# A decoder layer in fp32: tokens and context also handed over feature-major, one bank for new keys and values, gathers spread over the heads

## The chip, the cores and the metric

The kernel runs on one core of one Trainium2 chip. The metric is the device time of one execution in microseconds (us), the median of several runs. PE is TensorE, DVE is VectorE, ACT is ScalarE, POOL is GpSimd; SP and ACT and POOL also issue DMA transfers. A profile is one execution recorded by the hardware profiler.

## The reference, cut to what matters

One decoder layer on 2048 tokens (32 sequences of 64) of width 512: self-attention, cross-attention to a context of the same shape, and a feed-forward part, each followed by a layer norm.

```python
DIM, NH, NKV, HD = 512, 32, 8, 128
BLOCK, NBLK, TOPK = 32, 128, 16
q = rope(x @ wq.T); k = rope(x @ wk.T); v = x @ wv.T       # 32 query heads, 8 key heads
k_sel = k_cache[block_idx].reshape(-1, NKV, HD)            # 16 blocks of 32 rows = 512 cached keys
v_sel = v_cache[block_idx].reshape(-1, NKV, HD)
k_full = concatenate([k_sel, k[0]]); v_full = concatenate([v_sel, v[0]])   # + 64 new = 576 keys
attn = softmax(q @ k_full / sqrt(HD)); x = layernorm(x + (attn @ v_full) @ wo.T)
# cross-attention: q = x @ Wq + bq; k, v = split(context @ Wkv + bkv); per sequence of 64
x = layernorm(x + xattn(x, ctx) @ Wo + bo)
# feed-forward: z = x @ W.T + b, m = sum over 8 adapters of rank 16, z + min(0.5|z|/|m|, 1) * m
x = layernorm(x + ffn(x))
```

The new keys and values are those of the first sequence alone (`k[0]`, `v[0]`), and all 2048 tokens attend to the same 576 keys.

## The kernel before

Everything is fp32. The tokens are cut into four blocks of 512 (`NTB`), the heads into eight groups of four query heads that share one key head (`NKV`, `REP`). Self-attention is one long loop over `n`, 128 units of (group, token block, head). Its products with the large weights (queries, output projection) are done with seven quarter products instead of eight: a weight is loaded as four quarters, POOL makes the four sums that the scheme needs (`load_left`, `load_right`), POOL also makes four sums of the tokens (`token_sums`), and `Queries` and `Projection` issue the products 1 to 7 one at a time, in the order of `ORDER`.

In a unit, `scores(n, i)` is called four times, for 128 tokens each: two matmul pairs into a score bank (`s`, two banks in turn), DVE takes the row maximum (`nmax`), ACT the exponential and its sum (`p`, `den`), DVE the reciprocal, the multiplication of `p` and a 32 x 32 block transpose (`turn`, tile `T`). `move(n)` then has SP issue sixteen small transfers that bring `T` into the layout of `pT`, and two units later `values` multiplies it with `v` into the banks `po0` and `po1`. Between those matmuls, `step(place)` puts one query product of the next token block (`q_step`) or one output product of a past block (`w_step`) at each of four places of a unit: `steps = {0: "qwqw", 1: "qw q", 2: "wqwq", 3: "w qw"}[h]`. PE and DVE run in the order of the program, by hand; in the prologue (between `begin` and `begin.close()`) all engines do.

What the products need is the token matrix with features on the partitions (`xTs[tb]`), and it arrives token-major. So the kernel turns it on PE: `transpose_rows` does four 128 x 128 transposes against an identity into one bank and a copy by ACT or DVE out of it. For the first token block this is the beginning of the program; for blocks 1 to 3 the dictionary `early` spreads twelve such tiles over the first six units; every block is also written to DRAM (`xs`), and for later groups one transfer per block reads it back. The context is turned in the same way: four tiles in the last units (`pen0`), four after the loop (`en1`, bank `enbank`), eight in the key and value stage that follows (`rows_turn`, `pen2`, `pen3`).

Per group, when its second token block begins (`r == REP`), `gather_keys` and `gather_values` have POOL issue eight indirect transfers (four of keys, four of values, 128 rows each), `load_group` loads that group's key and value weights, `rotate` (a block later) applies the rotary factors on DVE and POOL, `new_keys` computes the new keys and values on PE, and `cached_keys` transposes the rotated keys on PE. `new_keys` uses the PSUM bank tag `po1` twice, once for the keys, read by ACT (L574), once for the values, read by ACT (L585).

When the output projection of a group's last token block has done its seventh product, `w_step` loads the next group's output weights into the same tiles: `load_right` issues four quarter loads on SP, then four POOL sums. The next group's first product (`w_0x`, `w_1x`... are banks of product 1 and 2 of block 0, 1...) is about three quarters of a unit later.

After the loop, `kv0` makes the keys and values of the first context block while the last output projections end. The key and value stage, cross-attention and the feed-forward part follow; the change touches the first of these only.

Of the kernel before, what the change touches and what calls it, by code (L numbers as in the profile page):

```python
# [16 lines left out]
P = 128  # L17
# [35 lines left out]
def decoder_layer(  # L53
# [3 lines left out]
    enc: bass.AP,  # L57
# [44 lines left out]
    def token_room(b, name):  # L102
        return act.tile([P, NC, TB], F32, tag=f"xT{b % 2}", name=name)

# [111 lines left out]
    def load_right(src, name, eng, queue=nc.sync):  # L216

        w = operands("wo", name)
        b12 = w[5]
        for dst, (k, n) in ((w[1], (0, 0)), (w[2], (1, 0)), (w[3], (1, 1)), (b12, (0, 1))):  # L220
            load_quarter(dst, src, k, n, queue)
        right_sums(eng, w[1], b12, w[2], w[3], {1: w[5], 2: w[6], 3: w[7], 4: w[4]})
        return w
# [191 lines left out]
    xs = [dram.tile([P, NC, TB], F32, name=f"xs{tb}") for tb in range(NTB)]  # L415
# [29 lines left out]
    def load_enc(tile_, tb, j):  # L445
        r0 = tb * TB + j * P
        nc.sync.dma_start(out=tile_, in_=enc[r0 : r0 + P, :])

# [6 lines left out]
    with ExitStack() as ph:  # L455
# [13 lines left out]
        blk = kc.tile([P, TOPK], I32, name="blk")  # L469
        nc.sync.dma_start(out=blk, in_=block_idx.partition_broadcast(P))  # L470
        for j in range(TPB):
            (nc.scalar if j % 2 else nc.sync).dma_start(
                out=acc[0][:, j, :], in_=x[j * P : (j + 1) * P, :]
            )
        wq0 = operands("wq", "wq0")
        for i, (k, m), queue in (
            (1, (0, 0), nc.sync), (4, (1, 1), nc.scalar),
            (5, (0, 1), nc.sync), (2, (1, 0), nc.scalar),
        ):
            load_quarter(wq0[i], wqT[:, : REP * HD], k, m, queue)  # L480
# [7 lines left out]
        NQ = P // BLOCK  # L488
        NKT = NSEL // P
        off_i = kc.tile([P, 1], I32, name="off_i")  # L490
        for q in range(NQ):
            nc.gpsimd.iota(
                off_i[q * BLOCK : (q + 1) * BLOCK, :], pattern=[[0, 1]], base=0,
                channel_multiplier=1,
            )
# [3 lines left out]
        blk_f = kc.tile([P, TOPK], F32, name="blk_f")  # L499
        nc.vector.tensor_copy(blk_f, blk)  # L500
        row_f = kc.tile([P, NKT], F32, name="row_f")
        for q in range(NQ):
            r = slice(q * BLOCK, (q + 1) * BLOCK)
            nc.vector.tensor_scalar(
                row_f[r, :], blk_f[r, :].rearrange("p (t q) -> p t q", q=NQ)[:, :, q],
                float(BLOCK * NKV), off[r, :], ALU.mult, ALU.add,
            )
        k_rows = k_cache.rearrange("n (h d) -> (n h) d", d=HD)
        v_rows = v_cache.rearrange("n (h d) -> (n h) d", d=HD)
        rows_cur, kn_cur, wkv_cur, kTs, vs = {}, {}, {}, {}, {}  # L510
# [11 lines left out]
        def gather_rows(g, dst, src):  # L522
            for t in range(NKT):
                nc.gpsimd.indirect_dma_start(
                    out=dst[:, t, :], out_offset=None, in_=src,
                    in_offset=bass.IndirectOffsetOnAxis(ap=rows_cur[g][:, t : t + 1], axis=0),
                )

        def gather_keys(g):
            rows_cur[g] = kv.tile([P, NKT], I32, tag="row", name=f"row{g}")  # L530
            nc.vector.tensor_scalar(rows_cur[g], row_f, float(g), None, ALU.add)
            kn_cur[g] = kv.tile([P, NKT, HD], F32, tag="kn", name=f"kn{g}", bufs=1)
            gather_rows(g, kn_cur[g], k_rows)

        def gather_values(g):
            vs[g] = kv.tile([P, NKC, HD], F32, tag="v", name=f"v{g}")
            gather_rows(g, vs[g], v_rows)

        def rotate(g):


            kn = kn_cur.pop(g).rearrange("p t (d two) -> p t d two", two=2)
            kr = kv.tile([P, NKT, HD], F32, tag="kr", name=f"kr{g}", bufs=1)
            k4 = kr.rearrange("p t (d two) -> p t d two", two=2)
            shape = [P, NKT, HD // 2]
            c3 = cs[:, None, :].to_broadcast(shape)
            s3 = sn[:, None, :].to_broadcast(shape)
            tmp = kv.tile(shape, F32, tag="tmp", name=f"kt{g}", bufs=1)
            tmq = kv.tile(shape, F32, tag="tmq", name=f"kq{g}", bufs=1)
# [7 lines left out]
            return kr  # L557
# [3 lines left out]
        def new_keys(g, tags=("po1", "po1")):  # L561

            wk, wv = wkv_cur.pop(g)
            src = xTs[0] if g == 0 else x64
            kTs[g] = kv.tile([P, NKEY], F32, tag="kT", name=f"kT{g}")
            pk = bank([P, 1, TB], f"pkn{g}", tags[0])[:, 0, :]
            for c in range(NC):
                nc.tensor.matmul(  # L570
                    pk[:, :SEQ], wk[:, c, :], src[:, c, :SEQ],
                    start=(c == 0), stop=(c == NC - 1),
                )
            nc.scalar.activation(  # L574
                kTs[g].rearrange("p (s b k) -> p s b k", s=2, k=SQ)[:, :, SHARED, :],
                pk[:, :SEQ].rearrange("p (s k) -> p s k", s=2), AF.Copy, scale=nrm2,
            )
            pv = bank([P, 1, TB], f"pvn{g}", tags[1])[:, 0, :]
            for c in range(NC):
                for i in range(2):  # L580
                    nc.tensor.matmul(
                        pv[i * SEQ : (i + 1) * SEQ, :HD], src[:, c, :SEQ], wv[:, c, :],
                        start=(c == 0), stop=(c == NC - 1), skip_group_check=True,
                    )
            nc.scalar.copy(vs[g][:, NKT, :], pv[:, :HD])  # L585

        def cached_keys(g, kr, tag="po1"):
# [13 lines left out]
        xTs = {}  # L601
# [86 lines left out]
        wq_cur, wo_cur, tok, qrs, pjs, reads = {}, {}, {}, {}, {}, []  # L688
        ORDER = (1, 2, 6, 7, 4, 5, 3)
# [12 lines left out]
        def q_step(n):  # L702

            b = n // REP + 1
            if b < NB:
                if b not in qrs:
                    start_queries(b, {k: "q" for k in "xyz"})
                    qrs[b].todo = list(ORDER)
# [3 lines left out]
                if i == 5:  # L712
                    reads.append(qrs[b].corner)

        def w_step(b):
# [5 lines left out]
            pj.step(pj.todo.pop(0))  # L721
            reads.append(pj.read)
            if not pj.todo:
                del pjs[b]
                g, tb, _ = units[b * REP]
                if tb == NTB - 1:
                    wo_cur[g + 1] = load_right(woT[columns(g + 1), :], f"wo{g + 1}", nc.gpsimd)
# [11 lines left out]
        for i in range(2):  # L739
            special[f"s{i}"] = sc.tile([P, 2, 512], F32, tag="sc", name=f"startbank{i}")[:, 0, :]  # L740
        xTs[0] = token_room(0, "xT0")

        def first_tile(j, tag):
            transpose_rows(acc[0][:, j, :], xTs[0], j, f"x_0_{j}", tag)

        sub = ALU.subtract
        q = {(i, j): xTs[0][:, quarter(i, j)[0], quarter(i, j)[1]]
             for i in range(2) for j in range(2)}
        t = {i: big.tile([P, 2, HF], F32, tag=f"tx{i}", name=f"tx0_{i}") for i in range(1, 5)}
        gather_keys(0)  # L750
        for j, tag in enumerate(("q", "w", "po0", "po1")):
            first_tile(j, tag)
        nc.vector.tensor_tensor(t[1], q[0, 1], q[0, 0], sub)
        nc.vector.tensor_tensor(t[2], q[1, 1], t[1], sub)
        nc.vector.tensor_tensor(wq0[7], wq0[1], wq0[5], sub)
        nc.vector.tensor_tensor(wq0[5], wq0[5], wq0[4], ALU.add)
        nc.vector.tensor_tensor(wq0[6], wq0[5], wq0[1], sub)
        wq_cur[0] = wq0
# [8 lines left out]
        nc.scalar.dma_start(out=acc[1], in_=rows(x, 1))  # L767
# [578 lines left out]
```

## Time and profile before

| | |
|---|---|
| median of 3 runs | 3136.03 us (3135.63 to 3137.8) |
| the profiled execution | 3155.39 us; its span from first to last instruction 3153.6 us |
| granted TensorE clock over the span | 0.994 |
| PE busy | 3081.5 us (98%) |
| DVE busy | 2200.4 us (70%) |
| POOL busy | 973.7 us (31%) |
| ACT busy | 771.2 us (24%) |

Durations of single instructions come from the profiled execution, whose own time is 19.4 us above the median. A line of a wait list names who waited, on what line, for whom, and then the total in us, the number of times and the longest. A line of the timeline has the start in us from the span's beginning, a length, engine, line, operation, output tile and inputs, shape and count; in brackets, how long the engine was idle before it and what released it. Matmuls are pipelined: what one costs is the time from its start to the next start. A wait for several semaphores is put down to the one that came last by the profile, so the name of a releaser can be wrong.

### The profile page before, as it was taken

The numbers are of one execution on the slowest core, as the hardware profiler recorded it, in microseconds if no ns is written. First come the engines' busy times: TensorE is split into PE (matmuls) and PEld (weight loads), VectorE is DVE, ScalarE is ACT, GpSimd is POOL, SyncE is SP. The second block draws the span as 40 slices with busy tenths as digits, with TensorE's granted clock in tenths as the row PEclk, the third lists the DMA queues.
The fourth block names the chain that finished last, engine by engine and source line by source line (L and its number), as shares of the span: only waits on it lengthen the run. The fifth ranks groups of instructions, "written<-read, shape, count | busy, mean of one in ns | idle before, by whom it ended". The sixth has DMA issues, their size and how long they took to land.

```text
span 3153.6 us, 42581 instructions
## 1 busy us (share of the span) xinstructions
PE 3081.5 (98%) x15072; PEld 2332.0 (74%) x15072; DVE 2200.4 (70%) x3945; ACT 771.2 (24%) x1782; POOL 973.7 (31%) x793
## 2 busy tenths in 40 slices
PE   8999999999999999999999999999999999999998
PEld 6677677677677676776777769988888888888864
DVE  6677777777777777777777754436666666656777
ACT  3323223222222222232232322211111111111122
POOL 3222222232222222223222113135434434444421
PEclk9999999999999999999999999999999999999999
DMA  5444444444444444444344443221121121121101
GB/s 186 118 113 113 118 107 122 111 113 113 115 122 108 115 125 109 104 127 115 96 125 110 111 114 121 107 94 48 54 61 50 52 61 52 49 65 50 48 27 41
DMA packets 187315, 298.70 MB, mean 95 GB/s; under 512 B 44128, under 2 KB 92768, under 8 KB 183008
## 3 DMA queue, kind: packets, MB, share of 16 engines
q1 hardware_dynamic: 173600, 281.46, 33.3%
q10 hardware_dynamic: 11072, 9.26, 1.0%
q0 software_dynamic: 2432, 5.26, 0.6%
q8 instruction: 122, 2.00, 0.3%
q14 instruction: 89, 0.73, 0.1%
HBM read 102.86 MB, written 25.17 MB: 41 GB/s over the span
## 4 chain that ended last, share of the span: by engine, by line
PE 91%; DVE 5%; SPq 1%; ACT 1%; issue 1%; DMA 1%; another core or an unknown queue 0%; ACTq 0%; DVEq 0%
PE po L656 15%; PE s L610 15%; PE sx L1068 2%; PE pox L1120 2%; PE wx_0y L268 1%; PE wx_2y L268 1%; PE wx_1y L268 1%; PE w_0y L268 1%; PE w_1y L268 1%; PE q_3y L268 1%; PE qx_3y L268 1%; PE qx_0y L268 1%; PE w_3y L268 1%; PE wx_3y L268 1%; PE q_1y L268 1%; PE q_0y L268 1%
## 5 line engine op out<-in xcount | busy, mean ns | idle before, releaser
L618 ACT ACTIVATE p<-s,nmax 128x576 f32<-128x576 f32 x512 | 379.8, 742 | 1186.2 <-DVE nmax L615 1145.9
L610 PE MATMUL s<-kT,qT 128*128 128x288 f32 x2048 | 579.0, 408 | 1.3 <-ACT p L618 1.3
L656 PE MATMUL po<-pT,v 128*128 128x512 f32 (+1 forms) x1280 | 551.9, 605 | 2.0 <-DVE encT L125 1.0
L610 PEld LDWEIGHTS s<-kT,qT 128*128 128x128 f32 x2048 | 388.3, 191 | 100.5 <-issue 19.1
L615 DVE TENSOR_REDUCE nmax<-s 128x1 f32<-128x576 f32 x512 | 384.3, 751 | 83.0 <-PE s L610 63.6
L636 DVE STREAM_TRANSPOSE T<-p 128x576 f32<-128x576 f32 x512 | 394.4, 770 | 4.4
L656 PEld LDWEIGHTS po<-pT,v 128*128 128x128 f32 (+1 forms) x1280 | 214.8, 190 | 203.2 <-issue 173.5
L628 DVE TENSOR_SCALAR p<-p,den 128x576 f32<-128x576 f32 x512 | 310.9, 607 | 17.9
L242 POOL TENSOR_TENSOR so<-oT,oT 128x512 f32<-128x512 f32 x32 | 42.4, 1326 | 726.3 <-ACT oT L679 726.3
L627 DVE RECIPROCAL den<-den 128x1 f32<-128x1 f32 x512 | 83.9, 164 | 236.2 <-ACT p L618 227.9
L244 POOL TENSOR_TENSOR so<-oT 128x512 f32<-128x512 f32 x32 | 40.7, 1273 | 320.3 <-PE w_1y L268 83.1
L1078 ACT ACTIVATE ex<-ex 128x512 f32<-128x512 f32 x64 | 40.4, 631 | 328.1 <-DVE ex L1077 328.1
L191 POOL TENSOR_TENSOR tx<-xT 128x512 f32<-128x512 f32 x31 | 39.8, 1283 | 236.6 <-PE q_1z L268 68.6
L1224 POOL TENSOR_TENSOR txx<-x1T 128x512 f32<-128x512 f32 x31 | 39.4, 1270 | 237.0 <-PE qx_3z L268 95.7
L618 ACT ACTIVATION_READ_ACCUMULATOR p<-s,nmax 128x1 f32 x512 | 99.0, 193 | 0.0
L1137 DVE TENSOR_SCALAR oTx<-pox,bv 128x256 f32<-128x256 f32 x128 | 56.1, 479 | 50.0 <-PE pox L1120 50.0
L242 POOL TENSOR_TENSOR sox<-oTx,oTx 128x512 f32<-128x512 f32 x32 | 40.5, 1267 | 156.8 <-DVE oTx L1137 151.8
L679 ACT COPY oT<-po 128x512 f32<-128x512 f32 x128 | 71.9, 587 | 43.5 <-PE po L656 42.5
L1068 PEld LDWEIGHTS sx<-kvx,qTx 128*64 128x64 f32 x2048 | 64.8, 138 | 20.9 <-issue 11.3
L1120 PE MATMUL pox<-pTx,kvx 64*128 64x256 f32 x512 | 74.5, 407 | 2.3 <-DMA pTx<-Tx 1.7
L1135 ACT ACTIVATE oTx<-pox,bv 128x256 f32<-128x256 f32 x128 | 53.8, 471 | 82.8 <-PE pox L1120 82.8
L1068 PE MATMUL sx<-kvx,qTx 128*64 128x64 f32 x2048 | 73.5, 225 | 0.0
(472 smaller groups left out, 5855.0 us busy)
## 6 DMA issues: line engine op xcount, KB each, us to landing
pT<-T SPq DMA_DIRECT2D x1020, 80.0 KB
pT<-T SPq DMA_DIRECT2D x1016, 64.0 KB
xT<-xs SPq DMA_DIRECT2D x28, 1024.0 KB
kvx<-kv SPq DMA_DIRECT2D x32, 512.0 KB
pTx<-Tx SPq DMA_DIRECT2D x256, 64.0 KB
kv<-c SPq DMA_DIRECT2D x30, 512.0 KB
xwq<-in_xwq SPq DMA_DIRECT2D x32, 256.0 KB
xwo<-in_xwo SPq DMA_DIRECT2D x32, 256.0 KB
```

What stands on the lines that cost most here:

```text
L242: nc.gpsimd.tensor_tensor(t[1], a[1, 0], a[1, 1], ALU.add)
L268: nc.tensor.matmul(self.banks[b][:, m, :], self.left[i][:, k, m * P : (m + 1) * P], self.right[i][:, k, :], start=(first and m + k == 0), ...
L610: nc.tensor.matmul(s[:, a, :HALF], qTs[n // REP][:, units[n][2], i * P : (i + 1) * P], kTs[g][:, a * HALF : (a + 1) * HALF], start=True, s ...
L615: nc.vector.tensor_reduce(nmax, s[:, :, :HALF], AX.XY, ALU.max, negate=True)
L618: nc.scalar.activation(p.rearrange("q (a k) -> q a k", a=2), s[:, :, :HALF], AF.Exp, bias=nmax, accum_out=den,)
L627: nc.vector.reciprocal(den, den)
L628: nc.vector.tensor_scalar(p, p, den, None, ALU.mult)
L636: nc.vector.transpose(Ts[n][:, :, i, :], ps_.pop((n, i)).rearrange("q (b k) -> q b k", k=SQ))
L656: nc.tensor.matmul(pos[n].rearrange("d (a q) -> d a q", a=NQD), vs[units[n][0]][rows, v, :], pTs[n // 2][rows, :, chunk, :], skip_group_ch ...
L679: nc.scalar.copy(o[:, i, :].rearrange("d (t a k) -> d a t k", t=TPB, a=NQD), pos.pop(n - 1 + i).rearrange("d (a t k) -> d a t k", a=NQD, t ...
L1068: nc.tensor.matmul(s[b * SEQ : (b + 1) * SEQ, i * REP + h, :], qTs[n][:, h, c0 : c0 + SEQ], kvs[n][:, pr, 0, c0 - pr * HF : c0 - pr * HF + ...
L1120: nc.tensor.matmul(po[b][:, i, :].rearrange("d (h a j) -> d h a j", h=REP, a=2), kvs[n][r, pr, 1, i * HD : (i + 1) * HD], pTs[n][r, :, t * ...
```

## The change

The host hands over `x` and the context transposed as well (`xT_in`, `encT_in`, 512 x 2048); `x` itself is still read for the residual sum. The index of the blocks is laid out on the host as 128 x 4.

- No tile of `x` or of the context is transposed on PE any more, `xs` and its stores are gone, and `load_features` loads a token block or context block as one transfer with features on the partitions.
- The prologue loads the first token block in quarters, makes the sums in another order, rotates the first keys in two halves, and leaves query product 3 to the first unit; products of the first two blocks stand at other places of the first three units, and block 1's use the bank tag `w` as well.
- `new_keys` puts new keys and new values into one bank, and ACT reads both after all matmuls.
- `load_right` is split: the first two quarters of the next group's output weights are loaded when products 1 and 2 of the group's last block are done, the other two when all seven are.
- The gathers go one per head: a key gather at the beginning and a value gather after the third score tile of each of the second block's four heads.
- At the end of self-attention the last products of `kv0` and the first two of the last projection alternate.

The core of the diff:

```diff
+    def load_features(dst, src, tb, queue=nc.sync):
+        queue.dma_start(
+            out=dst, in_=src[:, tb * TB : (tb + 1) * TB].rearrange("(c p) n -> p c n", p=P)
+        )
...
+    def load_right(src, name, eng, queue=nc.sync, first=None):
+        w = first or load_right_first(src, name, queue)
+        for i in range(3, 8):
+            w[i] = big.tile([P, 2, HF], F32, tag=f"wo{i}", name=f"{name}_{i}")
         b12 = w[5]
-        for dst, (k, n) in ((w[1], (0, 0)), (w[2], (1, 0)), (w[3], (1, 1)), (b12, (0, 1))):
+        for dst, (k, n) in ((w[3], (1, 1)), (b12, (0, 1))):
             load_quarter(dst, src, k, n, queue)
         right_sums(eng, w[1], b12, w[2], w[3], {1: w[5], 2: w[6], 3: w[7], 4: w[4]})
+        return w
+
+    def load_right_first(src, name, queue=nc.sync):
+        w = {i: big.tile([P, 2, HF], F32, tag=f"wo{i}", name=f"{name}_{i}") for i in (1, 2)}
+        for i in (1, 2):
+            load_quarter(w[i], src, i - 1, 0, queue)
         return w
...
+        for i, j, n, (k, m) in ((0, 0, 1, (0, 0)), (1, 0, 2, (1, 0)), (0, 1, 5, (0, 1)), (1, 1, 4, (1, 1))):
+            load_quarter(q[i, j], xT_in, i, j, (nc.sync, nc.scalar)[i and j])
+            load_quarter(wq0[n], wqT[:, : REP * HD], k, m, (nc.scalar, nc.sync)[n == 5])
...
-            pk = bank([P, 1, TB], f"pkn{g}", tags[0])[:, 0, :]
+            new = bank([P, 1, TB], f"new{g}", "po1")[:, 0, :]
+            pk, pv = new[:, :SEQ], new[:, P : 2 * P]
             (key matmuls)
-            (ACT reads the keys)
-            pv = bank([P, 1, TB], f"pvn{g}", tags[1])[:, 0, :]
             (value matmuls)
+            (ACT reads the keys)
             (ACT reads the values)
...
         def w_step(b):
...
+            if tb == NTB - 1 and g + 1 < NKV:
+                src, name = woT[columns(g + 1), :], f"wo{g + 1}"
+                if i == 2:
+                    wo_next[g + 1] = load_right_first(src, name)
+                if not pj.todo:
+                    wo_cur[g + 1] = load_right(src, name, nc.gpsimd, first=wo_next.pop(g + 1))
...
+        new_keys(0)
+        rotate(0, 0, NKT // 2)
+        nc.vector.tensor_tensor(c[1, 1], z, c[1, 0], ALU.add)
+        nc.vector.tensor_tensor(c[0, 1], y, c[1, 0], ALU.add)
+        rotate(0, NKT // 2, NKT)
+        for j in range(NKT):
+            gather_values(0, j)
+        cached_keys(0, "s0")
...
+        tok[1] = token_sums(xTs[1], "tx1", nc.gpsimd)
+        wo_cur[0] = load_right(woT[columns(0), :], "wo0", nc.gpsimd, first=wo_cur[0])
+        for tb in range(NTB):
+            (nc.scalar if tb else nc.sync).dma_start(out=acc[tb], in_=rows(x, tb))
...
             if r == REP and g + 1 < NKV:
-                gather_keys(g + 1)
-                gather_values(g + 1)
                 load_group(g + 1)
+            if r // REP == 1 and g + 1 < NKV:
+                gather_keys(g + 1, h)
...
+                if n < REP:
+                    i = {(0, 0): 3, (0, 1): 7, (0, 3): 4}.get((n, place))
+                    if i:
+                        last_products(i)
+                    elif (n, place) in ((0, 2), (1, 0), (1, 1), (1, 2), (1, 3), (2, 0), (2, 2)):
+                        q_step(n)
...
             step(2)
-            early_tiles(n, 2)
+            if r // REP == 1 and g + 1 < NKV:
+                gather_values(g + 1, h)
             scores(n, 3)
...
-                if NTB <= b + 3 < NB:
-                    xTs[b + 3] = token_room(b + 3, f"xT{b + 3}")
-                    nc.sync.dma_start(out=xTs[b + 3], in_=xs[units[(b + 3) * REP][1]])
+            if h == REP - 1 and b + 3 < NB or n == 0:
+                b2 = b + 3 if n else 2
+                xTs[b2] = token_room(b2, f"xT{b2}")
+                load_features(xTs[b2], xT_in, b2 % NTB)
...
-        kv_step(4, 3)
-        store_kv(0, 0, tiles)
-        spare2 = sc.tile([P, 2, 512], F32, tag="sc", name="enbank")
-        for j in range(TPB):
-            special["en"] = spare2[:, j % 2, :]
-            transpose_rows(en1[j], encT[1], j, f"pen1_{j}", "en")
+        pj.step(1)
+        pj.read()
+        kv_step(4)
+        pj.step(2)
+        pj.read()
+        kv_step(3)
+        store_kv(0, 0, tiles)
         encR[1] = token_sums(encT[1], "te1", nc.gpsimd, tag="so")
-        for i in KV_ORDER:
+        for i in (6, 5, 7, 3, 4):
```

Lines in parentheses stand for matmul loops and reads that are unchanged in themselves.

## The prediction

> **What bounds the kernel now.** I read the page first (shares, chain), then who waited for whom on PE, then the timeline and the stretches around each wait.
>
> ```profile
> span 3153.6 us, 42581 instructions
> PE 3081.5 (98%) x15072; PEld 2332.0 (74%) x15072; DVE 2200.4 (70%) x3945; ACT 771.2 (24%) x1782; POOL 973.7 (31%) x793
> PE 91%; DVE 5%; SPq 1%; ACT 1%; issue 1%; DMA 1%; another core or an unknown queue 0%; ACTq 0%; DVEq 0%
> ```
>
> TensorE is the chain (91%). So two things are worth time: matmul work that goes, and moments in which PE stands. The list of waits has nearly all of those moments:
>
> ```profile
> PE pvn L581 <- ACT kT L574: 11.9, 7, 1.7
> PE x L123 <- ACT xT L125: 10.6, 2, 5.3
> PE x L123 <- DMA acc<-in_x: 6.7, 1, 6.7
> PE w_0x L268 <- DMA wo<-in_woT: 3.9, 3, 1.5
> PE w_0x L268 <- DVE nmax L615: 3.0, 2, 1.5
> PE w_0x L268 <- DVE den L627: 2.6, 1, 2.6
> ```
>
> Columns: total us, times, longest. The change touches every row. Next the stretches (length, then busy time of PE, PEld, DVE, ACT, POOL, granted clock, DMA share, GB/s), for the first block of tokens (four heads), the start of the second, and one whole group of later work:
>
> ```profile
> 22.70:77.20 54.50, 46.44 (x191) 33.86 (x189) 42.37 (x71) 18.47 (x42) 20.86 (x20) 0.94 0.56 169
> 77.20:97.00 19.80, 14.47 (x55) 9.92 (x54) 10.64 (x20) 7.09 (x16) 9.96 (x10) 0.83 0.32 87
> 97.00:328.00 231.00, 229.31 (x907) 164.15 (x906) 176.53 (x313) 67.98 (x158) 55.81 (x46) 1.00 0.45 115
> 372.00:376.60 4.60, 4.45 (x22) 3.04 (x23) 1.71 (x4) 0.61 (x3) 0.00 (x0) 0.63 0.57 160
> ```
>
> The later group is PE-bound (229 of 231 us, DVE 177). The first 97 us are not: PE idles there and the clock falls (0.94, 0.83).
>
> **The change part by part.** The sum is made against the profiled execution, 3155.39 us; the median of the runs shown is 3136.03, 19.4 us less. I carry that difference over unchanged.
>
> *1. Token and context transposes go.* PE loses 32 tiles of four transposes: 16 of tokens, 16 of context. The 16 tiles of x1 stay. What a tile costs on PE is the start of its successor minus its own start:
>
> ```profile
> 82.66 0.60 PE L123 MATMUL x<-ident,acc 128*128 128x128 f32 x4
> 83.10 1.14 PE L610 MATMUL s<-kT,qT 128*128 128x288 f32 x4
> 92.69 0.90 PE L123 MATMUL x<-ident,acc 128*128 128x128 f32 x3 [5.33 <-ACT xT L125]
> ```
>
> 83.10 - 82.66 = 0.44 us. Twelve tiles lie in the first 97 us (items 4 and 5), 8 at the end of self-attention (item 6), and 8 in the key and value stage, where PE is never idle (1930 to 2096: 166.0 of 166.0): 8 x 0.44 = 3.5 us gained there. Their ACT and DVE copies were beside PE work: nothing.
>
> *2. New keys and values in one bank.* At each of seven groups PE waited between the key and the value products, because both used the tag po1:
>
> ```profile
> 139.97 1.00 PE L570 MATMUL pkn<-x,wk 128*128 128x64 f32 x8
> 142.67 1.09 PE L581 MATMUL pvn<-wv,x 128*64 128x128 f32 x16 [1.70 <-ACT kT L574]
> ```
>
> Eight matmuls of 0.105 us end near 140.8; the next start is 142.67: 1.86 us, seven times, 13.0 us. In the new order both products are issued before the ACT reads, and po1 is next written a head later, so nothing takes the wait's place. Two of the seven waits were followed by about 3.4 us at half clock (the row of 372.00 to 376.60 shows 0.63), 1.7 us lost each. The Trainium skill ("TensorE: Matmul & The Clock Gate", section on HAM oscillation) speaks against counting these: PE should avoid idle gaps above about 3.4 us, and 1.7 us is below. By rule 13.0 us, by trace 16.4. I take the trace, with 13.0 in the range.
>
> *3. Output weights in two steps.* SP now loads the first two quarters of the next wo after product 2 of the group's last block, some 3.5 heads (about 50 us) earlier; SP only waits there for that product, with nothing due behind it before the head's own move. Before, all four stood behind the sixteen moves of a head:
>
> ```profile
> 797.91 1.13 PE L610 MATMUL s<-kT,qT 128*128 128x288 f32 x4
> 801.62 1.97 PE L268 MATMUL w_0x<-wo,oT 128*128 128x256 f32 x8 [2.57 <-DVE den L627]
> ```
>
> The releaser named is wrong: it is the load, issued at 798.4. The three w_0x rows sum to 9.5 us in six waits; all go. What is late next are POOL's sums for product 6, due about 13 us later; they needed until 809.9 before, from a landing that now holds two loads instead of four. No new wait: 9.5 us.
>
> *4. Prologue and first block.* Before, the first scores started at 22.7 and those of the second block at 77.2. Now: the eight quarter loads are as many bytes as the tiles and weights before, and share their 8 DMA lanes, so product 1 starts as the transposes did, at 6.7. At half clock it takes 3.4, the ACT copy 0.6, product 2 2.0: 12.8. Then two products at 1.73, new keys and values 1.9: 18.1. DVE: six sums at 0.69 after the last weight quarter (about 11.5), 0.6 of small ones, two half rotations of about 1.5, two adds of 0.69: 19.8. Then transposes 0.6 and two ACT copies: first scores at about 21. This gains 1.7 although product 3 now comes after. The four heads hold 16 score pairs at 0.97, ten products at 1.73 and 8.0 of values, 40.8 us of PE. DVE has 4 x (0.75 + 0.16 + 0.61 + 0.77) = 9.2 a head and eight adds, 42.1 us. So DVE binds here; with 5 us for the links between engines the second block starts near 68, 9 us earlier. What made 54.5 us of this before was one DVE instruction:
>
> ```profile
> 40.38 3.76 DVE L628 TENSOR_SCALAR p<-p,den 128x576 f32<-128x576 f32 x1
> 41.32 1.28 POOL L190 TENSOR_TENSOR tx<-xT 128x512 f32<-128x512 f32 x1
> 46.76 0.47 PE L123 MATMUL x<-ident,acc 128*128 128x128 f32 x1 [5.30 <-ACT xT L125]
> ```
>
> It usually takes 0.52; ACT, then the tile's copy, then PE waited behind it. The Trainium skill ("GPSIMD Engine Reference", Specifications) says GpSimd shares its SBUF interfaces with VectorE and contends with two-port or two-input DVE instructions. This speaks against the change: eight POOL sums stand in a row (10 us), about 23 to 33, beside the DVE-bound heads. By rule each of some eight multiplies could wait one POOL sum, 8 x 1.28 = 10 us, and the 9 us are gone. By trace the mean multiply is 0.61 against 0.52. I take 0.61 and keep 0 as an end. The early loads (4 MB of rows, 3 of tokens) are at most 10.5 MB by about 36 us at the 330 GB/s seen here; the first values are due near 44. ACT's moves could wait 1 to 2 us on a lane: inside the 5 us.
>
> *5. Second block.* PE stood 5.33 us before a tile (row 92.69), then ran 6.8 us at half clock (3.4 lost); both hang on the tile's copy. With four tiles (1.8) that is 10.5 us. The seven late DVE reads at this place belong to the burst of eight gathers:
>
> ```profile
> DVE nmax L615 <- remote: 16.6, 7, 5.4
> ```
>
> In the other six groups PE lost nothing there. One pair of gathers per head moves 64 POOL issues of about 1 us off that burst, with three more row additions of 0.15 us on DVE a group; DVE has 50 us free in a group: nothing.
>
> *6. End of self-attention.* Eight tiles (3.5), the idle time between the last four (0.68 + 0.85 + 0.68 = 2.2), their half clock (w_3x took 2.85 against 1.89, and 0.5 in the tile: 1.5), and about 1.7 of waits on tile copies and on a value read that a reordered product now covers: 8.9 us. The single 1 MB loads of context start after the last readers of their room, 15 us or more ahead of use.
>
> *7. Feature-major loads each block.* They replace loads of the stored copy, at the same place on SP. Pieces are 2 KB instead of 8. The row loads of x have the same pieces and reached 360 GB/s; a block has four heads of slack: nothing. If they came later, the moves behind them on reused lanes would be late.
>
> Sum: 3.5 + 16.4 + 9.5 + 9 + 10.5 + 8.9 = 57.8 us. 3155.4 - 57.8 = 3097.6 in a profiled execution; 3136.0 - 57.8 = 3078.2 in the median. I say 3079.
>
> **The rivals.** *A. The start gives nothing* (DVE beside POOL, and half of item 5 comes back as DVE-bound waits): less 9 and 8.7: gain 40, 3096. For it: the multiply of 3.76. Against: DVE was busy only 42.4 of 54.5. *B. The early stalls belong to the profiled execution*, which is 19.4 us longer than the median: 5.3 + 3.4 of item 5 and as much of item 4 would not be in the median: again about 3096. *C. Slower: the gathers.* Late signals beside the gather burst (1.2 to 5.4 us) cost PE 5.3 us once. If each of the 28 heads that now gathers stopped PE so, 28 x 5.3 = 149 us, 3136 - 58 + 149 = 3227. It decides from 2.1 us a head. Against: no PE loss in six of seven bursts, and two gathers are not eight.
>
> **How the numbers follow.** Main case 0.70, its own range 3060 to 3094 (item 2 by rule, item 4 from 0 to 14). A 0.14, B 0.10, C 0.05, no measurable change 0.01. To hold eight in ten the range reaches over A and B: 3060 to 3102. 0.2% is 6.3 us, about what a measurement can tell here: faster 0.94, same 0.01, slower 0.05.
>
> **What would show it.** Right: no PE wait between new-key and value products; w_0x without idle time; 128 fewer L123 matmuls; second block's scores near 68; clock 1.0 from 30 us to the end of self-attention. Wrong: PE waits on POOL sums at product 6 (item 3), on pT moves in the third head (item 4), or on DVE or ACT beside gathers (C); multiplies of over 1 us in a row in the first two heads (A).

## The result and the profile after

The changed kernel takes 3111.0 us in the median (3105.07 to 3111.14, 4 runs), the kernel before 3135.83 (3129.73 to 3137.8, 4 runs): ratio 0.9919, 95% interval 0.9902 to 0.9937, 24.8 us less. The forecast was 3079. The profiled execution of after takes 3110.9 us, which is its own median; that of before was 19.4 us above its median. Between the spans of the two profiles lie 44.6 us, between the timed runs 24.8.

The page of after, then who waited for whom on PE:

```profile
span 3109.0 us, 42300 instructions
PE 3059.1 (98%) x14944; PEld 2312.8 (74%) x14944; DVE 2199.3 (71%) x3957; ACT 757.3 (24%) x1760; POOL 971.6 (31%) x789
PE 91%; DVE 4%; DMA 2%; SPq 2%; ACT 1%; issue 1%; ACTq 0%; DVEq 0%
```

```profile
PE s L615 <- ACT p L623: 10.8, 10, 1.2
PE q_0x L282 <- DMA xT<-in_xT: 4.9, 1, 4.9
PE po L661 <- DMA pT<-T: 4.6, 5, 2.1
PE q_1z L282 <- DVE qT L299: 2.9, 1, 2.9
```

The 128 transposes of x and the context are gone (14944 matmuls instead of 15072), and so are the rows `pvn` and `w_0x` and those of tiles turned on PE out of `acc`. The first row is new in its size: ten waits of score matmuls for ACT, 10.8 us, where before there was one of 1.3. The stretches that answer to those of before (first block, start of the second, a later group):

```profile
19.60:73.00 53.40, 46.78 (x164) 33.29 (x164) 38.54 (x68) 13.42 (x32) 19.28 (x17) 0.90 0.63 190
73.00:93.00 20.00, 19.42 (x73) 13.40 (x72) 15.94 (x34) 7.94 (x18) 5.14 (x5) 1.00 0.46 117
93.00:321.00 228.00, 227.71 (x897) 162.37 (x897) 176.82 (x319) 67.72 (x158) 55.98 (x46) 1.00 0.45 115
```

The first block still takes 53.4 us (54.5 before), at a clock of 0.90. In the start of the second block PE is busy for 19.42 of 20.00 us.

The kernel before was timed in five comparisons. In four its median was 3133 to 3136 us, in one 3157.5 (17 runs, 3153.4 to 3163.1); the profile from which the forecast was made took 3155.4 us, though the runs timed with it took 3136, and shows the stalls of that long kind (experiment 1). Below, "short" and "long" name these two. A half-clock window is a stretch of about 3.4 us in which the profile shows a granted clock of 0.5; each costs half its length, 1.7 us.

### The profile page after: what moved, and what is told of

Read it like the earlier page. It is cut to its first block, busy times and chain, and to the rows that moved or that the text cites. A ratio compares the mean times of both kernels' runs of the same rounds, so it can differ in the third digit from the quotient of the medians.

```text
span 3109.0 us, 42300 instructions
## 1 busy us (share of the span) xinstructions
PE 3059.1 (98%) x14944; PEld 2312.8 (74%) x14944; DVE 2199.3 (71%) x3957; ACT 757.3 (24%) x1760; POOL 971.6 (31%) x789
## 3 DMA queue, kind: packets, MB, share of 16 engines
q0 software_dynamic: 2048, 4.20, 0.5%
## 4 chain that ended last, share of the span: by engine, by line
PE 91%; DVE 4%; DMA 2%; SPq 2%; ACT 1%; issue 1%; ACTq 0%; DVEq 0%
PE po L661 15%; PE s L615 15%; PE sx L1041 2%; PE pox L1093 2%; PE wx_0y L282 1%; PE wx_2y L282 1%; PE wx_1y L282 1%; SPq L653 1%; PE w_0y L282 1%; PE q_3y L282 1%; PE w_3y L282 1%; PE qx_0y L282 1%; PE qx_3y L282 1%; PE wx_3y L282 1%; PE q_2y L282 1%; PE w_1y L282 1%
## 5 line engine op out<-in xcount | busy, mean ns | idle before, releaser
L615 PE MATMUL s<-kT,qT 128*128 128x288 f32 x2048 | 578.0, 408 | 11.6 <-ACT p L623 10.8
L633 DVE TENSOR_SCALAR p<-p,den 128x576 f32<-128x576 f32 x512 | 324.9, 635 | 17.9
```

The lines of the kernel that those rows point to most:

```text
L615: nc.tensor.matmul(s[:, a, :HALF], qTs[n // REP][:, units[n][2], i * P : (i + 1) * P], kTs[g][:, a * HALF : (a + 1) * HALF], start=True, s ...
L633: nc.vector.tensor_scalar(p, p, den, None, ALU.mult)
```

## The experiments

Experiments 1 to 4 ran on one chip, 5 to 8 on a second, 9 to 12 on a third, 13 to 16 on a fourth, each time with the kernel before beside them; only on the first was that kernel of the long kind.

**1. The kernel before, profiled again** (no edit).

> The kernel before, unchanged, profiled once more. The forecast gain of 57.8 us was read from one profiled execution of 3155.4 us, 19.4 above the median of its runs; the changed kernel was profiled at 3110.9 us, at its median of 3111.0. Theory 1 (stalls that only that execution had): a second profile is near 3136 to 3140 us, and the stalls near 41 us (DVE multiply of 3.76 us), near 87 us (PE 5.33 us idle) or the half clock near 2124 us are gone or much smaller, 10 to 19 us in all. Theory 2 (the profiler itself adds 19 us to every execution of this kernel): again 3153 to 3157 us with the same stalls at the same places. Time against before: ratio 1.000 within 0.001.

3156.6 us (12 runs), ratio 0.9999 (0.9991 to 1.0008); profiled at 3164.1. The stalls of the first profile were there again (PE before `x` 10.5 us in two waits, `w_0x` 9.7). So neither theory as written: the stalls are not those of one execution, and the profiler does not add them to every execution (experiment 9 is profiled at 3131.9). All runs of this comparison are long.

**2. One bank for new keys and values alone** (groups 1 to 7).

```diff
-            pk = bank([P, 1, TB], f"pkn{g}", "po1")[:, 0, :]
-            (key products; ACT reads) ; pv = bank(..., "po1"); (value products; ACT reads)
+            new = bank([P, 1, TB], f"new{g}", "po1")[:, 0, :]
+            (key products; value products; ACT reads both)
```

> The kernel before with one edit of the change: new keys and values of groups 1 to 7 in one bank, both read after all products. By the sum of the prediction 13.0 us less (seven waits at 1.86), 16.4 with the two half-clock windows: 3120 to 3123 from 3136. If those waits are filled later (PE then waits elsewhere for ACT or DVE as much): within 3 us of before. The wait of PE on ACT kT is gone from the profile in either case.

3138.5 us against 3157.5: ratio 0.9942 (0.9929 to 0.9956), 18 to 19 us. The wait is gone, and with it every half-clock window between 97 and 2100 us (three in the profile from which the forecast was made, seven in experiment 1's).

**3. Output weights in two steps alone.**

```diff
-            if not pj.todo: wo_cur[g + 1] = load_right(...)
+            if i == 2: wo_next[g + 1] = load_right_first(...)
+            if not pj.todo: wo_cur[g + 1] = load_right(..., first=wo_next.pop(g + 1))
```

> The kernel before with one edit: the first two quarters of the next output weights are loaded after product 2 instead of after product 7 of the group's last block. The prediction: 9.5 us less (six waits before w_0x). Rival: given back within a unit, as in the changed kernel, where the offset went from -13.78 to -15.24 and back to -13.77 us at one group: then 0 to 1 us less. With the gathers still in one burst at the block's start, the long multiply (2.97 us) should not appear at this place, and if it is the gathers that take the gain, 9 us stay.

3140.1 us: ratio 0.9949 (0.9935 to 0.9963), some 17 us. The waits before `w_0x` are gone, nothing is given back, and one half-clock window is left between 97 and 2100 us. Each of experiments 2 and 3 gave more than its own waits (12 and 9.5 us).

**4. The changed kernel with the gathers in one burst again.**

```diff
-            if r // REP == 1 and g + 1 < NKV: gather_keys(g + 1, h)    (and gather_values after tile 3)
+            if r == REP and g + 1 < NKV:
+                for t in range(NKT): gather_keys(g + 1, t)
+                for t in range(NKT): gather_values(g + 1, t)
```

> The changed kernel with one edit undone: the eight gathers of a group in one burst at the start of the second block, as before, instead of two per head. If the gathers of head 3 beside POOL sums hold the multiply of 2.97 us and with it PE for 1.37 us in six groups, this is 8 us faster than the changed kernel (3103), and the six waits of score matmuls on ACT of 1.2 us are gone. If the sums alone do it, the waits stay and the time is that of the changed kernel within 2 us. If the burst costs something of its own (late DVE reads, the stall near 87 us comes back), slower by 5 to 9 us.

3103.4 us, ratio 0.9827 (0.9813 to 0.984), 54 us below the long kernel before. The six waits of score matmuls in the later groups are gone. DVE still waits for signals marked "remote", which means that the profile finds no releaser on this core. Such waits are the mark of the long kind (16.6 us in the prediction's row of the same form), and smaller here:

```profile
DVE nmax L620 <- remote: 6.0, 5, 1.9
```

**5. The changed kernel again** (no edit).

> The changed kernel, unchanged, beside the kernel before on one chip, because the kernel before took 3136 us in the runs first shown and 3157.5 us (17 runs) beside experiments 1 to 4. Theory 1 (clock windows: a window of 3.41 us in which PE stood for over about 2.1 us is followed by one at half clock, 1.7 us lost; the kernel before has 13 waits of 1.5 to 1.9 us that fall on either side of that, the changed kernel six of 1.4 us that stay below): the changed kernel is at 3103 to 3112 us whatever the kernel before does; if the kernel before is again near 3157, the gain is 46 to 54 us, ratio 0.983 to 0.985. Theory 2 (these executions are all longer by a common amount): the changed kernel is near 3131 and the gain 25 us, ratio 0.992.

3109.8 us against 3133.8: ratio 0.9924 (0.991 to 0.9938). The changed kernel is where it was. The kernel before was short this time, so the two theories, which differ only where it is long, stay undecided.

**6. Bank and output weights together.** The edits of 2 and 3.

> The kernel before with both edits of experiments 2 and 3. Each alone gave about 18 us against the kernel before (0.9942 and 0.9949), though their own waits are 13.0 and 9.5 us. If the waits and their clock windows add, 36 us less: 3121 to 3122. If the first of the two already takes the half-clock windows away (theory 1: body windows 7 in the kernel before profiled again, 0 and 1 in the two), the second adds only its own waits: 13.0 + 9.5 + some 8 to 12 of windows = 30 to 34 us less than 3157, so 3123 to 3127, and the body from 97 to 2100 us shows no half clock. The w_0x gain is kept here because the gathers are in one burst.

3117.5 us against 3133.8: ratio 0.9951 (0.9937 to 0.9964), 16 us less, not the 30 to 34 expected beside a long kernel before. No half clock between 12 and 2087 us. Together they give no more here than either alone gave beside the long kernel.

**7. The rest of the change alone:** the kernel of experiment 4 with bank and output weights as before.

> The rest of the change alone: feature-major loads, the new prologue and first three units, the new end of self-attention; new keys and values of groups 1 to 7, output weights and gathers as before. By the profiles of before and after (first scores to unit 5: 12.9 us; end of self-attention 7.0; key and value stage 3.7) 22 to 24 us less than before, if the number of half-clock windows in between does not change; with all 13 waits of the loop kept, the windows stay (3 to 7 of them in the body) and the time is 3132 to 3136 where before is 3157. The prediction's items 1, 4, 5 and 6 sum to 31.9.

3119.3 us against 3133.8: ratio 0.9956 (0.9943 to 0.997), 14.5 us. The wait `w_0x` is absent from its profile, though its loads are those of before.

**8. The kernel of experiment 4 with late row loads.**

```diff
-        for tb in range(NTB): (nc.scalar if tb else nc.sync).dma_start(out=acc[tb], in_=rows(x, tb))
+            if n == REP - 1:
+                for tb in range(NTB): nc.sync.dma_start(out=acc[tb], in_=rows(x, tb))
```

> The changed kernel with the gathers in one burst (experiment 4) and the loads of the four row blocks of x (4 MB, needed first by the output projections near 97 us) issued after the fourth unit instead of in the prologue. In the changed kernel ACT's second move of the first unit was blocked on a transfer until 38.5 us, its exponential waited 2.94 us, PE then 1.23, 1.19 and 2.86 us and fell to half clock twice. If these loads are what delays it: the second block's first scores move from 70.3 to 63 to 66 us and the kernel is 4 to 8 us faster than experiment 4 (3095 to 3099). If DVE (multiplies of 1.1 to 1.6 us beside POOL sums) sets the pace: less than 2 us.

3099.3 us, ratio 0.9891 (0.9876 to 0.9906). The second block's first scores are at 68.7 instead of 70.3 and 71.4 (experiments 4 and 11), not at the 63 to 66 expected. So the loads were a small part of what holds the start; PE still waited 3.8 us for DVE to read the bank of product 5.

**9. The kernel before, profiled a third time** (no edit).

> The kernel before, unchanged, profiled a third time. Its runs were near 3134 us in two comparisons and near 3157 us in one, while both profiles so far (3155 and 3164 us) belong to the long kind. If this profile is of the short kind (3128 to 3138 us): the first block runs as in experiment 6, second block's fifth unit near 87 us instead of 96.8 (10 us less), no PE wait before w_0x or half of the 9.5 us, and no more than two half-clock windows between 97 and 1800 us. If these three do not account for 20 us, the missing difference lies elsewhere. If it is of the long kind (3153 to 3163), the stalls of the first profile are there again.

3133.1 us (10 runs), ratio 1.0001 (0.9992 to 1.001), its profile 3131.9: short. Its row for the start of the second block, and its PE waits in full down to 1.6 us:

```profile
78.00:98.00 20.00, 20.00 (x82) 13.23 (x81) 15.70 (x29) 9.30 (x22) 7.95 (x8) 1.00 0.52 129
```

```profile
PE pvn L581 <- ACT kT L574: 11.9, 7, 1.7
PE x L123 <- DMA acc<-in_x: 6.5, 1, 6.5
PE x L123 <- ACT xT L125: 3.8, 2, 3.1
PE x L123 <- ACT x1T L125: 2.4, 3, 1.5
PE pu L1174 <- DVE gam L1201: 1.8, 1, 1.8
PE s L610 <- ACT p L618: 1.6, 2, 1.3
```

PE is busy for all of 78 to 98 us (14.47 of 19.80 us in the prediction's row for this place), and no `w_0x` row is left. Both have one origin. In the long kind, DVE's signals come late beside the burst of eight gathers (the timeline of before, DVE, in the second block):

```profile
92.11 0.76 DVE L615 TENSOR_REDUCE nmax<-s 128x1 f32<-128x576 f32 x1 [5.37 <-remote]
```

No profile beside a short kernel before has such a wait, with the burst or without it; all five that are of the long kind or were taken beside it have them (experiment 4 among these). In the long kind, DVE ends the unit of the burst 16.98 to 17.35 us after its first scores, in the short one (experiment 9) 14.22 to 14.23, in six groups each (19.6 and 14.2 in the first). SP's sixteen moves stand behind that, and the output weights behind the moves. The timeline of SP at group 3 in the long profile (the prediction shows the product that follows, at 801.62):

```profile
787.17 11.19 SPq L648 DMA_DIRECT2D pT<-T  x16
798.40 2.15 SPq L197 DMA_DIRECT2D wo<-in_woT  x4
```

The same in the short one, SP and then PE:

```profile
781.52 2.15 SPq L197 DMA_DIRECT2D wo<-in_woT  x4
```

```profile
785.29 1.89 PE L268 MATMUL w_0x<-wo,oT 128*128 128x256 f32 x8
```

In all six groups of the long profile the product starts 3.2 us after the first of the four loads is issued, and some 1.6 us of that PE was idle (9.5 us in six waits): it was due 1.6 us after the issue. In the short one it starts 3.5 to 4.6 us after the issue, with no idle time. The load is issued later against PE's work. Experiment 4 agrees: there DVE also ends the burst's unit late (16.5 to 17.6 us, 13.5 to 14.2 in experiment 11), but the output weights are loaded early, and it takes the same 3103.4 us as experiment 11.

**10. The changed kernel a third time** (no edit).

> The changed kernel, unchanged, beside experiment 4's kernel and the kernel before on one chip. 3105 to 3112 us on a chip of either kind; ratio 0.992 where the kernel before is near 3134, 0.985 where it is near 3157.

3111.3 us against 3133.4: 0.9928 (0.9911 to 0.9944).

**11. The kernel of experiment 4 beside it.**

> The changed kernel with the eight gathers of a group in one burst again (experiment 4, which ran beside the kernel before alone). On the same chip as the changed kernel: 6 to 9 us less (six waits of score matmuls of 1.37 us and what the first block does), so 3100 to 3104. If the difference of experiment 4 to the changed kernel was one of chips: within 2 us of it.

3103.4 us, 7.9 below the changed kernel on the same chip. In the changed kernel one multiply of `p` per group lasts 2.97 us; here it does not, and the six waits behind it are gone. First POOL and DVE in the fourth head of the second block of the changed kernel, with the score matmul that waited:

```profile
341.31 0.96 POOL L523 DMA_INDIRECT kn<-in_k_cache,row  x1 [0.59 <-DVE row L538]
342.58 0.94 POOL L523 DMA_INDIRECT v<-in_v_cache,row  x1 [0.30 <-issue]
343.54 1.28 POOL L199 TENSOR_TENSOR tx<-xT,tx 128x512 f32<-128x512 f32 x1
344.77 0.74 POOL L557 TENSOR_TENSOR kr<-kn,cs 128x256 f32<-128x256 f32 x1
```

```profile
342.86 2.97 DVE L633 TENSOR_SCALAR p<-p,den 128x576 f32<-128x576 f32 x1
```

```profile
348.07 1.24 PE L615 MATMUL s<-kT,qT 128*128 128x288 f32 x4 [1.20 <-ACT p L623]
```

Then the same place in experiment 11:

```profile
339.19 1.27 POOL L199 TENSOR_TENSOR tx<-xT,tx 128x512 f32<-128x512 f32 x1
```

```profile
339.62 1.16 DVE L633 TENSOR_SCALAR p<-p,den 128x576 f32<-128x576 f32 x1
```

The multiply lasts until POOL's unbroken row of instructions ends: 345.83 against POOL's 345.51 in the changed kernel, 340.78 against 340.46 here. (The multiply of 3.76 us in the prediction's item 4 ended at 44.14, POOL's row beside it at 43.82: also 0.32 us apart.) Two gathers push one sum and the first rotation into its way, and the row is three instructions long instead of one. With the burst, the rotation's first step on POOL comes right behind it, three heads earlier. The same multiply took 2.96 to 2.97 us in all six later groups, in each of four profiles of the changed kernel.

**12. Experiment 8's kernel with products 3 and 4 of the second block one place later.**

```diff
-    ... (1, 3), (2, 0), (2, 2)): q_step(n)
+    ... (1, 3), (2, 1), (2, 3)): q_step(n)
```

> Experiment 8's kernel (gathers in one burst, rows of x loaded after the fourth unit) with query products 3 and 4 of the second block one place later in the third unit, (2, 1) and (2, 3) instead of (2, 0) and (2, 2). In experiment 8 product 3 waited 3.84 us at 44 us for DVE to read the bank of product 5, and a half-clock window followed. If PE is held by that order: 3 to 6 us less than experiment 8 (3093 to 3096). If DVE sets the pace of the first four units: less than 1 us.

3098.6 us (3095.8 to 3101.9), ratio 0.9892 (0.9876 to 0.9909): below experiment 11 on the same chip by 4.9, with experiment 8 within 1 us. In its profiled execution (3095.8) the second block's scores stand at 65.8, and the first block is at full clock:

```profile
19.90:65.80 45.90, 42.09 (x165) 30.10 (x165) 36.70 (x68) 13.43 (x32) 19.20 (x17) 1.00 0.74 223
```

The median does not show those 3 us, so what the place of the two products is worth stays open. This is the fastest version: 12.7 us below the changed kernel on the same chip.

**13. The kernel before with the gathers one per head alone** (and, as in the change, a row addition of 0.13 us on DVE ahead of each key gather).

```diff
-                gather_keys(g + 1); gather_values(g + 1)
+            if r // REP == 1 and g + 1 < NKV: gather_key(g + 1, h)     (and gather_value after tile 3)
```

> The kernel before with one edit: one key gather and one value gather per head of the second block, and one row addition per head, instead of eight gathers at the block's start. Where the kernel before is near 3134 us (no late signals beside the burst, no PE wait before w_0x): what head 3's pair does in the changed kernel, 1.3 to 1.5 us in each of six groups, so 8 to 9 us more (3142), as experiment 11 gives with the opposite sign. Where it is near 3157 (DVE ends the burst's head 2.8 us late, the moves and the output weights then come later, PE waits before w_0x and in the second block): those waits go, 9.5 + 8 to 10 us, the multiply still costs 8 to 9, so 8 to 14 us less. If the gathers cost nothing (the prediction): within 2 us of 3134, or 18 to 20 us less than 3157.

3157.0 us against 3133.9: ratio 1.0078 (1.0064 to 1.0092), 23 us more, beyond the 8 to 9 expected. Its PE waits:

```profile
PE pvn L600 <- ACT kT L593: 18.2, 7, 2.8
PE s L629 <- ACT p L637: 8.9, 8, 1.3
```

The score waits are the 8 to 9 us. On top, six of the seven waits for the bank `po1` grew from 1.7 to 2.7 us: DVE is still late a head further on, so the exponential ahead of ACT's read of the new keys is late. And each of the seven was now followed by a half-clock window (two in experiment 9). By trace that is 7.3 + 6.3 + 5 x 1.7 = 22 us. The changed kernel has no such wait on the bank, so there the gathers cost little beside the score waits (7.9 us, experiment 11).

**14. Bank alone, the kernel before short** (experiment 2's kernel).

> Experiment 2's kernel (bank alone) again, because experiment 2 ran where the kernel before was near 3157. Near 3134 it should take 7 x 1.77 = 12.4 us and the half-clock windows that those waits set off (two or three, 1.7 us each): 13 to 18 us less, 3116 to 3121. The w_0x rows show no wait of PE. If it is near 3157 again: 19 us less as in experiment 2.

3119.0 us against 3133.9: ratio 0.9953 (0.9939 to 0.9967), 14.9 us.

**15. Output weights alone, the kernel before short** (experiment 3's kernel).

> Experiment 3's kernel (output weights in two steps alone) again. Near 3134 the kernel before has no PE wait before w_0x (third profile: load issued 4.6 us ahead of the product instead of 3.2), so this edit gives 0 to 2 us. If the edit still gives 9 us or more, the explanation of the missing gain by that wait is wrong. Near 3157: 17 us less as in experiment 3.

3133.6 us (13 runs) against 3133.9: ratio 0.9998 (0.999 to 1.0006). Nothing is gained, as expected from the short profile.

**16. The changed kernel a fourth time** (no edit).

> The changed kernel, unchanged, on the same chip as experiments 13 to 15. Where the kernel before is near 3134: ratio 0.992 to 0.993, as three times so far. Where it is near 3157: 3105 to 3114 us, ratio 0.983 to 0.986, since its profile has no wait that late signals could lengthen by more than a few us (the burst is gone and the output weights are loaded early).

3110.2 us against 3133.9: 0.9926 (0.9911 to 0.9941). What the changed kernel itself takes where the kernel before is long was not measured; the nearest is experiment 4, with 3103.4 us there and 3103.4 elsewhere (experiment 11).

## Why the prediction was wrong

The direction was right and the mechanisms existed. Three steps failed: the 19.4 us carried over unchanged (18.8 us of items 3 and 5 are not in the runs), "one pair of gathers per head: nothing" (7.9 us lost), and item 4, sized at 9 us and found at about 2. Point by point, with the short profile (experiment 9) as the base:

- **The base.** "I carry that difference over unchanged" supposed that the 19.4 us had nothing to do with the terms of the sum. They were in the terms: second block and `w_0x`, whose waits the short kind does not have. Rival B had it right that the runs lack stalls of the profile, but gave it one chance in ten and saw only the early ones. "In the other six groups PE lost nothing there" was a misreading: the late signals of those six groups are what makes the output weights late, the six waits of item 3.
- **Item 1** (key and value stage): 3.5 forecast, 3.7 found. (Its count is off without effect: sixteen token tiles are turned, fifteen of them before 97 us, and 32 tiles of x1 stay, not 16.)
- **Item 2:** 16.4 forecast, 14.9 found alone (experiment 14). The wait costs about what was said (experiment 14's expectation has 1.77 us, seven times, 12.4), and half-clock windows come on top. "By trace" was the right choice, though the number of windows changes with the execution.
- **Item 3:** 9.5 forecast, 0.3 found (experiment 15). The three rows were real in the profile, but belong to the long kind, where the edit gives 17 (experiment 3).
- **Item 4:** 9 forecast. The second block's scores were to be near 68 instead of 77.2. In four profiles of the changed kernel they are at 70.4 to 73.1, and in the short kernel before already at 73.9: 1 to 3.5 us less. All of this lies ahead of the first scores (19.5 to 20.3 instead of 22.8; 21 forecast). The four heads, forecast at 47 us, take 50.2 to 53.4, and took 51.1 in the short kernel before: nothing gained. The "5 us for the links between engines" were too few. Three rows of the changed kernel, ACT and then PE:

```profile
39.10 0.74 ACT L623 ACTIVATE p<-s,nmax 128x576 f32<-128x576 f32 x1 [2.94 <-DMA pT<-T]
```

```profile
39.98 1.24 PE L615 MATMUL s<-kT,qT 128*128 128x288 f32 x4 [1.23 <-ACT p L623]
...
49.83 3.78 PE L282 MATMUL q_1z<-xT,wq 128*128 128x256 f32 x8 [2.86 <-DVE qT L299]
```

  An exponential stood behind a move of ACT's own queue, and product 3 needs the bank of product 5, which DVE reads late; then PE ran at half clock, at 42 and 49 us. Rival A named this place, but with POOL as its cause; late loads and product order are worth about 5 us together (experiment 12 against 11). What else holds the four heads is not shown.
- **Item 5:** 10.5 forecast, 0.9 found: in the short profile units 4 to 7 take 52.6 us, in the changed kernel 51.7. The 5.33 us of idle time came with the late signals: the short kind turns the same tiles and has no such wait.
- **The gathers:** nothing forecast, 7.9 us lost (experiment 11), in the kernel before 23 (experiment 13). "DVE has 50 us free in a group" is a sum over the group. The place counts: in the fourth head the pair stands against a POOL sum and the rotation, and of 2.45 us more on one multiply 1.2 reach PE through ACT within a head. Rival C had the sign and the gathers, but the wrong mechanism (late signals, of which the profiles with pairs show none).
- **Item 6:** 8.9 forecast, 7.7 found. **Item 7:** nothing, as forecast.

The found terms sum to 3.7 + 14.9 + 0.3 + 2.2 (the middle of item 4) + 0.9 - 7.9 + 7.7 = 21.8, beside 22 to 25 in the four comparisons. The timed experiments add up as well: items 2 and 3 together gave 16.2 us (experiment 6), items 1, 4, 5 and 6 together 14.5 (experiment 7), 30.7 in all; experiment 11, which has them all with the burst, gave 30.0. The forecast of 57.8 is close to the 54 us of experiment 4 beside the long kernel, but by luck in part: the gathers' loss is not in experiment 4, and item 4 gave less than was said.

What makes runs long or short, and why signals come late beside the burst there, stays open: the trace names no releaser, each comparison ran on another chip, so that chip and occasion are not told apart, and no run here changes the kind.

## What to carry to other kernels

When the profiled execution is far from the median of the runs, do not carry the difference over: the stalls that you mean to remove may be the difference, so profile the kernel before a second and a third time and price only the waits that all of them have. What a moved POOL instruction cost here lay not in its own length but in its neighbours: before one is moved, look at what POOL does just before and after, and whether a DVE multiply on the chain falls into that unbroken row. Recurring waits of 1.7 us on PE were worth more than their length here, because some of them, and all of them once a small delay was added, were followed by a window at half clock.

## What the runs showed of the hardware that was not expected

The half clock is given in windows of 3.41 us on a fixed grid, whose place differs from execution to execution. In 18 profiles, between 100 and 1780 us, 24 windows at half clock follow one at full clock, and ahead of each of these 24 stands a window in which PE was busy for 1.81 us or less; of 8795 windows that no half clock followed, seven were as empty. The limit is not sharp in these profiles, and the 2.1 us of experiment 5's expectation is only near it: counted by the starts of the matmuls (what is more than the median distance for their shape, above 60 ns), 1.77 us or more stood empty ahead of each half clock, and up to 2.09 in windows that none followed. Two pairs of windows of the kernel before (experiment 9), then one of experiment 13; the columns are the window, its length, busy PE, PEld, DVE, ACT, POOL, clock, DMA share, GB/s:

```profile
1042.20:1045.60 3.40, 1.89 (x13) 1.62 (x11) 2.40 (x6) 1.50 (x4) 0.85 (x1) 1.00 0.47 109
1045.60:1049.00 3.40, 3.22 (x23) 2.29 (x24) 1.56 (x4) 0.46 (x3) 0.00 (x0) 1.00 0.48 141
1270.90:1274.30 3.40, 1.71 (x20) 1.54 (x20) 2.37 (x5) 1.62 (x4) 0.31 (x1) 1.00 0.33 81
1274.30:1277.70 3.40, 3.40 (x17) 2.49 (x14) 0.10 (x1) 0.27 (x1) 0.00 (x0) 0.50 0.47 137
```

```profile
361.50:364.90 3.40, 0.66 (x12) 0.54 (x12) 2.33 (x5) 1.04 (x3) 0.27 (x1) 1.00 0.47 109
364.90:368.30 3.40, 3.40 (x17) 2.37 (x12) 0.23 (x1) 0.27 (x1) 0.00 (x0) 0.51 0.55 164
```

The first pair has a wait of 1.7 us that reaches 0.2 us beyond the window, and stays at full clock with 1.89 us busy; the second has the same wait wholly inside the window, and falls with 1.71. So equal waits can cost differently: of seven waits of 1.7 us, two were followed by a half clock in experiment 9 and three in experiment 15. Grown to 2.7 us, as in the third pair, all six were. The Trainium skill ("TensorE: Matmul & The Clock Gate", Part 1 and HAM oscillation) has a free-running window of 3413 ns and a rule against idle gaps above some 3.4 us. The window agrees with these profiles; the limit does not: here about half a window without work was enough, in most cases.

The second is the multiply beside POOL. The Trainium skill ("SBUF — State Buffer", SBUF: two separate sides) says that a DVE instruction in a two-port mode or with two SBUF inputs, and a GpSimd instruction, take a shared pair of ports as a lock: whichever starts first has it for its whole instruction, and the other is blocked. That fits a wait for one POOL instruction. Here a 0.52 us multiply lasted through three POOL instructions in a row, 2.97 us, and ended 0.32 us after the last of them; that it was the lock which held it is not shown by a run.
